# Layer 0's first pass and its hand-overs rewritten: wider runs of x, a hand-made order, weight products inside the pass, early stores, tables in attention's pools

## The chip, the cores and the metric

The kernel runs on one core of one Trainium2 chip. Times are microseconds of device time for one execution. Engines are named as the profile names them: PE is TensorE's matmul side and PEld its weight loads, DVE is VectorE, ACT is ScalarE, POOL is GpSimd, and SP is SyncE, which issues nearly all DMAs in one queue, in order. A matmul holds one operand still (the weights, `lhsT`) and streams the other (`rhs`) through it.

## What is computed

x is a float32 image of 256 by 256 tokens with 128 channels (32 MB). Four layers follow one another, each of the form x = x + f(gn(x)), where gn is a group norm over the whole image. Only layer 0 and the start of layer 1 matter here.

```python
def _gn(v, G=32, eps=1e-5):
    g = v.reshape(B_, H_, W_, G, C_ // G)
    m = jnp.mean(g, axis=(1, 2, 4), keepdims=True)
    s = jnp.var(g, axis=(1, 2, 4), keepdims=True)
    return ((g - m) / jnp.sqrt(s + eps)).reshape(v.shape)
...
def _L0_conv_ref(x, mask, ln_w, ln_b, w_tri, w_q, w_k, w_v, w_g, b_g, w_o, b_o):
    xn = (x - mu) * jax.lax.rsqrt(var + EPS) * ln_w + ln_b      # per token, over 128 channels
    tri_bias = jnp.einsum('bijd,dh->bhij', xn, w_tri)[:, None]
    mask_bias = INF * (mask[:, :, None, None, :] - 1.0)
    q = (xn @ w_q).reshape(B, I, J, H, C) * (1.0 / np.sqrt(C))  # k, v and the gate g alike
    scores = jnp.einsum('bimhc,binhc->bihmn', q, k) + tri_bias + mask_bias
    attn = jax.nn.softmax(scores, axis=-1)
    o = jnp.einsum('bihmn,binhc->bimhc', attn, v)
    return (g * o).reshape(B, I, J, H * C) @ w_o + b_o
...
x = x + _L0_conv_ref(_gn(x), ...)   # layer 0: attention along each of the 256 rows, 4 heads of 32
x = x + _L1_conv_ref(_gn(x), ...)   # layer 1: gated products of tokens, a triangle product
```

The group norm's mean and variance need all of x before the first normalised value exists. So layer 0 reads x once for the statistics and again for the work.

## The kernel before

The kernel keeps channels on the 128 partitions and tokens along the free axis. x arrives with tokens on partitions, so it is turned. Tokens go in 32 pieces of 2,048 (`SC`, 1 MB each); 512 tokens (`CK`) fill one PSUM bank of 2 KB per partition.

**First pass (L209 to L226).** For each piece, SP loads 1 MB of x (L214; each partition gets four runs of 2 KB), PE turns it in 16 transposes of 128x128 (L221, four for each PSUM bank), DVE takes `bn_stats` of the bank (L223) and ACT copies the bank to SBUF (L224). The last 14 pieces (18 to 31, `held`) stay in SBUF. The first 18 are stored to `xT` in DRAM (L226). Tile pools give the loads three buffers (tag `xt`), the copies three (tag `xs`) and PSUM six banks. The order on each engine is made by the framework's scheduler, which sends loads and stores in groups of four.

**Products of weights (L228 to L275).** Layer norm's scale and offset are folded into the weights of layers 0 and 2, in some 20 small matmuls and DVE copies through the pool `f0ps`. They stand behind the first pass, between the last `bn_stats` and the group norm.

**Group norm (L164 and `gn_groups`, L166 to L184).** `bn_aggr` joins the 128 groups of statistics, two small matmuls sum over the channels of a group, ACT takes the root and DVE the reciprocal. The folded weights `wf` and `wt` are scaled by it (L296 to L298).

**Second pass (L316 to L342).** Held and stored pieces alternate (`order`: 18, 0, 19, 1, ...), 32 in all. ACT squares the normalised piece (L321), PE forms five rows of it with `wt` (L324) and sums the squares into one bank (L342), DVE copies the rows out (L330), and SP stores them in four small DMAs (L336, `triD`). For a held piece SP also stores the 1 MB to `xT` (L332), for another it loads one of the next 1 MB pieces (L285, three buffers). The engines' order is written by hand here (`manual_schedule`).

**Hand-over to attention (L349 to L430).** The variance of each token is worked out from the two sums (L353 to L358), written to `rsD` and read back in two layouts. In the pool `p2i`, the bias table `triT` and the mask table `mbT` are loaded, scaled and turned by PE (L382 to L402). Only when `p2i` is closed do attention's pools open, and the first group of rows is loaded (L428, L430), normalised by ACT and POOL (L436, L437) and projected by PE (L464). From there to 1540 us the attention loop runs, unchanged by the diff.

**Hand-over to layer 1 (L638 to L720).** After attention the statistics are checked and joined, and small weights are folded (L664 to L697, pools `f1` and `f1ps`), among them `bz` and `wzc` from eight POOL selections. Then layer 1's first pass loads x1 in pieces of 1 MB (L707) and multiplies (L712). One piece in four is kept in SBUF.

Of the kernel before, what the change touches and what calls it, by code (L numbers as in the profile page):

```python
# [15 lines left out]
P = 128  # L16
# [15 lines left out]
def kernel(ctx: ExitStack, tc: tile.TileContext, a: dict, out: bass.AP):  # L32
# [127 lines left out]

    def gn_finish(stats, name):

        mv = const.tile([P, 2], F32, name=name + "_mv")
        nc.vector.bn_aggr(mv, stats.rearrange("p n s -> p (n s)"))  # L164
        return gn_groups(mv, name)
# [38 lines left out]
    w0c = const.tile([P, 4 * D + NH], F32, name="w0c")  # L204
    slide = const.tile([P, 63], F32, name="slide")
# [3 lines left out]
    with tc.tile_pool(name="x0", bufs=1) as xres, tc.tile_pool(name="p0", bufs=3) as sb:  # L209
        held = {s: xres.tile([P, SC], F32, name=f"x0_{s}") for s in range(RES, NSC)}  # L210
        with tc.tile_pool(name="p0ps", bufs=6, space=PSUM) as ps:
            for s in range(NSC):
                xt = sb.tile([P, 4, 4, D], F32, name="p0_x", tag="xt")
                nc.sync.dma_start(  # L214
                    xt, x_tok[s * SC : (s + 1) * SC, :].rearrange("(c p k) d -> p c k d", p=P, k=4)
                )
                xc = held[s] if s in held else sb.tile([P, SC], F32, name="p0_xc", tag="xs")
                for c in range(4):
                    pt = ps.tile([P, P, 4], F32, name="p0_t")
                    for k in range(4):  # L220
                        nc.tensor.transpose(pt[:, :, k], xt[:, c, k, :], ident)  # L221
                    pf = pt.rearrange("p n k -> p (n k)")
                    nc.vector.bn_stats(stats0[:, s * 4 + c, :], pf)  # L223
                    nc.scalar.copy(xc[:, c * CK : (c + 1) * CK], pf)  # L224
                if s not in held:
                    nc.sync.dma_start(xT[:, s * SC : (s + 1) * SC], xc)  # L226

        with tc.tile_pool(name="f0", bufs=1) as fsb, tc.tile_pool(name="f0ps", bufs=1, space=PSUM) as ps:  # L228
            cen = fsb.tile([P, P], F32, name="f0_c")
            nc.vector.tensor_scalar(cen, ident, -1.0 / D, None, ALU.add)  # L230
            wa = fsb.tile([P, 4 * D + NH], F32, name="f0_a")
            nc.vector.tensor_scalar(wa, w0, ln_w, None, ALU.mult)
            wb = fsb.tile([P, 4 * D + NH], F32, name="f0_b")
            nc.vector.tensor_scalar(wb, w0, ln_b, None, ALU.mult)
            for lo, hi in ((0, 4 * D), (4 * D, 4 * D + NH)):
                pc = ps.tile([P, hi - lo], F32, name="f0_pc", tag=f"f0_pc{lo}")
                nc.tensor.matmul(pc, lhsT=cen, rhs=wa[:, lo:hi], start=True, stop=True)
                nc.vector.tensor_copy(w0c[:, lo:hi], pc)
            pq = ps.tile([P, 3], F32, name="f0_pq")
            for j, i in enumerate((0, 1, 3)):  # L240
                nc.tensor.matmul(pq[:, j : j + 1], lhsT=w0[:, i * D : (i + 1) * D], rhs=ln_b, start=True, stop=True)
            nc.vector.tensor_copy(cqkg, pq)
            pv = ps.tile([P, D], F32, name="f0_pv")
            nc.tensor.matmul(pv, lhsT=ones, rhs=wb[:, 2 * D : 3 * D], start=True, stop=True)
            for k in range(4):
                nc.vector.tensor_copy(cv[:, k, :], pv)

            w2c_ = const.tile([P, 6, D], F32, name="w2c_")
            wa2 = fsb.tile([P, 6, D], F32, name="f0_a2")
            nc.vector.tensor_scalar(wa2[:, 0:5, :], w2[:, 0:5, :], lniw, None, ALU.mult)  # L250
            nc.vector.tensor_scalar(wa2[:, 5, :], w2[:, 5, :], lnow, None, ALU.mult)
            for lo, hi in ((0, 4), (4, 6)):
# [6 lines left out]
            for i in range(6):  # L259
                nc.tensor.matmul(  # L260
                    pb2[:, i : i + 1], lhsT=w2[:, i, :], rhs=lnib if i < 5 else lnob, start=True, stop=True
                )
# [1391 lines left out]
```

## Time and profile before

The median of three runs is 3493.68 us (3490.01 to 3493.93). The profiled execution took 3508.45 us, of which its instructions span 3506.8; it is 14.8 us (0.4%) above the median.

| What | In the profile |
|---|---|
| PE busy | 3133.7 us, 89% of the span, 20260 matmuls and 20260 weight loads |
| DVE, ACT, POOL busy | 66%, 56%, 46% |
| DMA | 759.49 MB, 217 GB/s on the mean |
| first pass, to the last statistics | 0 to 164.1 us |
| weight products and group norm | 164.1 to 175.3 us |
| second pass | 175.3 to 277.4 us |
| hand-over to the first projection | 277.4 to 309.6 us |
| attention | 309.6 to 1540.5 us |
| to layer 1's first matmul | 1540.5 to 1562.9 us |
| layers 1 to 3 | from there to 3506.8 us |

Busy time is the time in which an engine's instructions ran, and matmuls are pipelined, so a busy PE need not be at its peak. In the profile a float32 matmul that is not a transpose stands as two records, each with its own weight load: L464 is issued 384 times and has 768 records. A transpose stands as one: L221 is issued 512 times and has 512. "PEclk" is the TensorE clock granted, as a share of full speed; "DMA share" is the busy share of the core's 16 DMA engines.

### The profile page before, as it was taken

To read this page: it belongs to the slowest core of one execution; us is meant where nothing else is said; L and a number is where in the kernel's file an instruction comes from. 1 tells how busy PE (TensorE), PEld (TensorE's weight loads), DVE (VectorE), ACT (ScalarE), POOL (GpSimd) and SP (SyncE) were. 2 spreads that over 40 slices of the span, in tenths; PEclk is the share of its full clock that TensorE was granted. 3 is DMA by queue.
4 is the path that set the end of the run, shared out by engine and by line. 5 is a ranking of instruction groups with operands and counts; after the bars stand their busy time and mean duration, and the time that the engine had idled before them with its cause. 6 is when DMAs were issued, how large, how long until landed. Compare 5 with 4: busy or idle time off the path is not lost.

```text
span 3506.8 us, 52443 instructions
## 1 busy us (share of the span) xinstructions
PE 3133.7 (89%) x20260; PEld 1652.1 (47%) x20260; DVE 2321.5 (66%) x2637; ACT 1961.4 (56%) x2198; POOL 1605.4 (46%) x821
## 2 busy tenths in 40 slices
PE   3675999999999999966597899999999999959998
PEld 3512555555555555521432344444899533314444
DVE  4624888888888888852388454544555677747776
ACT  3563777777777777733243454443444466636655
POOL 4002777777777777732488000000555354514343
PEclk7887999999999999978799899999999999969999
DMA  9883333333333333349599686775999899747664
GB/s 334 324 317 113 98 123 114 106 122 115 105 122 111 109 122 112 108 156 387 173 321 356 228 312 244 284 270 193 342 353 351 307 335 322 277 168 204 193 200 133
DMA packets 309867, 759.49 MB, mean 217 GB/s; under 512 B 77627, under 2 KB 148957, under 8 KB 259437
## 3 DMA queue, kind: packets, MB, share of 16 engines
q1 hardware_dynamic: 298749, 746.43, 60.9%
q0 software_dynamic: 10864, 9.65, 0.9%
q8 instruction: 162, 2.65, 0.3%
q14 instruction: 92, 0.75, 0.1%
HBM read 468.28 MB, written 287.66 MB: 216 GB/s over the span
## 4 chain that ended last, share of the span: by engine, by line
PE 38%; DMA 7%; DVE 2%; ACT 1%; SPq 1%; issue 1%; POOL 0%; ACTq 0%; DVEq 0%; POOLq 0%
PE p_pm L946 13%; PE tp_z L1612 6%; PE p_pm L1099 4%; PE p_pm L1334 4%; PE p_pg L810 3%; DMA x3T<-p_x 2%; PE tp_a L1601 2%; PE p_st L903 1%; PE p_pt L1371 1%; PE p_pz L818 1%; DMA p_er<-eD 1%; DMA x2T<-p_x 1%; DMA p_x<-x3T 1%; PE p_eb L860 1%; PE p_rz L860 1%
## 5 line engine op out<-in xcount | busy, mean ns | idle before, releaser
L489 DVE TENSOR_TENSOR p_e<-p_S,triT 128x1024 f32<-128x1024 f32 x512 | 609.0, 1211 | 144.7 <-PE p_S L479 144.7
L499 POOL TENSOR_TENSOR p_es<-p_e 128x1024 f32<-128x1024 f32 x256 | 603.1, 2367 | 127.4 <-issue 67.3
L497 ACT ACTIVATE p_e<-p_e,mbT 128x1024 f32<-128x1024 f32 x512 | 551.8, 1137 | 63.0 <-DVE p_e L489 61.2
L946 PE MATMUL p_pm<-p_zn,wf 128*128 128x512 f32 x1040 | 450.0, 594 | 1.4 <-DVE p_zn L963 1.4
L464 PE MATMUL p_mm<-p_xn,wf 128*128 128x512 f32 x768 | 409.2, 617 | 9.2 <-POOL p_xn L437 9.2
L437 POOL TENSOR_TENSOR p_xn<-p_xn,p_rs 128x1024 f32<-128x1024 f32 x64 | 153.5, 2398 | 452.2 <-DMA p_rs<-rsD 259.9
L946 PEld LDWEIGHTS p_pm<-p_zn,wf 128*128 128x128 f32 x1040 | 197.6, 191 | 254.6 <-issue 247.8
L479 PE MATMUL p_S<-p_q,p_k 32*128 32x256 f32 x4096 | 295.4, 400 | 5.0 <-DVE p_e L489 5.0
L479 PEld LDWEIGHTS p_S<-p_q,p_k 32*128 32x128 f32 x4096 | 185.8, 184 | 161.5 <-PE p_mm L455 91.7
L1348 POOL TENSOR_TENSOR p_q<-p_q,p_pb 128x2024 f32<-128x2024 f32 x32 | 144.1, 4503 | 254.8 <-DVE p_pb L1342 254.8
L1612 PE MATMUL tp_z<-p_B,tp_at 128*128 128x256 f32 x1024 | 250.2, 387 | 2.4 <-DMA p_B<-bD 2.2
L512 PE MATMUL p_o<-p_e,p_v 128*32 128x256 f32 x4096 | 249.2, 384 | 0.0
L1012 POOL DMA_DIRECT2D rs__18024<-rs2D x4 | 2.1, 520 | 531.7 <-PE p_pm L946 531.7
L1055 POOL TENSOR_TENSOR k<-k,p_sq 128x512 f32<-128x512 f32 x128 | 163.1, 1274 | 135.2 <-ACT p_sq L1053 135.2
L1165 POOL TENSOR_TENSOR p_x<-p_x,p_g 128x2048 f32<-128x2048 f32 x30 | 136.2, 4542 | 171.9 <-DVE p_g L1152 137.8
L1612 PEld LDWEIGHTS tp_z<-p_B,tp_at 128*128 128x128 f32 x1024 | 185.1, 191 | 24.5 <-issue 2.5
L464 PEld LDWEIGHTS p_mm<-p_xn,wf 128*128 128x128 f32 x768 | 126.8, 191 | 114.6 <-issue 90.3
L1054 DVE TENSOR_TENSOR k<-tp_z,k 128x512 f32<-128x512 f32 x128 | 88.6, 692 | 128.4 <-ACT p_sq L1053 128.4
L512 PEld LDWEIGHTS p_o<-p_e,p_v 128*32 128x32 f32 x4096 | 120.4, 110 | 110.1 <-ACT p_g L470 41.5
L979 DVE SCALAR_TENSOR_TENSOR p_b<-p_pm,b2w,p_b 128x1024 f32<-128x1024 f32 x64 | 82.2, 1284 | 126.6 <-PE p_pm L946 112.2
L455 PEld LDWEIGHTS p_mm<-wf,p_xn 128*128 128x128 f32 x1024 | 135.3, 192 | 62.8 <-issue 61.9
L1051 ACT COPY p_K<-tp_z 128x512 f32<-128x512 f32 x128 | 74.9, 585 | 159.7 <-PE tp_z L1612 159.7
(353 smaller groups left out, 5903.8 us busy)
## 6 DMA issues: line engine op xcount, KB each, us to landing
p_x<-x2T SPq DMA_DIRECT2D x64, 1024.0 KB
p_x<-x1T SPq DMA_DIRECT2D x48, 1024.0 KB
p_x<-in_x_dram SPq DMA_DIRECT2D x32, 1024.0 KB
p_x<-xT SPq DMA_DIRECT2D x64, 512.0 KB
p_rs<-rsD SPq DMA_DIRECT2D x64, 512.0 KB
p_rb<-rzD SPq DMA_DIRECT2D x256, 128.0 KB
x1T<-p_x SPq DMA_DIRECT2D x64, 512.0 KB
aD<-p_a SPq DMA_DIRECT2D x32, 1024.0 KB
```

Of the source, the lines that this page charges most:

```text
L437: nc.gpsimd.tensor_tensor(xn, xn, t["rs"], ALU.mult)
L464: nc.tensor.matmul(pm, lhsT=w, rhs=t["xn"][:, cs_], start=True, stop=True)
L479: nc.tensor.matmul(Ss[h // 2][:, h % 2, u, :], lhsT=t["k"][hp, r * N + u * P : r * N + (u + 1) * P], rhs=t["q"][hp, r * N : (r + 1) * N], ...
L489: nc.vector.tensor_tensor(e[:, :, 2 * p : 2 * p + 2, :].rearrange("p u h n -> p h u n"), Ss[p], triT[:, 2 * p : 2 * p + 2, :, :], ALU.add,)
L497: nc.scalar.activation(e[:, u, :, :], e[:, u, :, :], AF.Exp, bias=mbT[:, u, i : i + 1])
L499: nc.gpsimd.tensor_tensor(es, e[:, 0, :, :], e[:, 1, :, :], ALU.add)
L512: nc.tensor.matmul(t["o"][hp, r % 2, :], lhsT=t["v"][:, r * 2 + u, hp], rhs=e[:, u, h, :], start=(u == 0), stop=(u == 1),)
L946: nc.tensor.matmul(pm[:, c, :], lhsT=wf2[:, i, :], rhs=zns[s][:, k * CK : (k + 1) * CK], start=True, stop=True)
L1055: nc.gpsimd.tensor_tensor(k2, k2, sq, ALU.add)
L1099: nc.tensor.matmul(pm[:, c, :], lhsT=w, rhs=src[:, k * CK : (k + 1) * CK], start=True, stop=True)
L1348: nc.gpsimd.tensor_tensor(q[:, :, 1 : N - 2], q[:, :, 1 : N - 2], pb[:, :, 0 : N - 3], ALU.add)
L1612: nc.tensor.matmul(pz[:, t, :], lhsT=at[:, u, t * P : (t + 1) * P], rhs=Bc[:, u, :], start=(u == 0), stop=(u == 1))
```

## The change

The first pass is written anew in a hand-made order. A piece is loaded as two blocks of 1,024 tokens, so that each partition's run is 4 KB. Three loads go ahead, and the load of piece s+3 is issued after piece s's PE work. A PSUM tile has two banks (three such tiles, in place of six of one bank), and holds 1,024 tokens whose order within the tile has a stride of eight. A turn of 128 tokens would cross the two banks, so it is done as two plain matmuls, with x as weights and one half of the identity (64 columns) as the moving operand: 32 matmuls for a piece in place of 16 transposes, 1,024 in all in place of 512. ACT copies both banks in one instruction. `bn_stats` stays at one bank.

The weight products (`folds`) are issued after piece 12's work, through two PSUM banks of their own, and with them layer 1's `bz` and `wzc`. The statistics of the first 124 groups are joined while the last piece is worked on (`gn_part`), and joined with the last four afterwards (`gn_merge`).

Held pieces 18 to 22 are stored to `xT` ahead of the group norm instead of within the second pass. The variance's offset and square become one ACT instruction. The tables `triT` and `mbT` are built in attention's own pools, so that on SP the first two loads of x for attention and the first `p_rs` go ahead of `tri`, `mk` and `rs`. Nothing else is changed: the attention loop and layers 1 to 3 have the same instructions.

```diff
+    def gn_part(stats, lo, hi, name):
+        mv = const.tile([P, 2], F32, name=name)
+        nc.vector.bn_aggr(mv, stats[:, lo:hi, :].rearrange("p n s -> p (n s)"))
+        return mv
...
+    def gn_merge(a, b, wa, name):
+        mv = const.tile([P, 2], F32, name=name)
+        d = const.tile([P, 2], F32, name=name + "_d")
+        nc.vector.tensor_tensor(d[:, 0:1], a[:, 0:1], b[:, 0:1], ALU.subtract)
+        nc.vector.scalar_tensor_tensor(mv[:, 0:1], d[:, 0:1], wa, b[:, 0:1], ALU.mult, ALU.add)
+        nc.vector.scalar_tensor_tensor(d[:, 1:2], d[:, 0:1], wa * (1 - wa), d[:, 0:1], ALU.mult, ALU.mult)
+        nc.vector.scalar_tensor_tensor(d[:, 1:2], a[:, 1:2], wa, d[:, 1:2], ALU.mult, ALU.add)
+        nc.vector.scalar_tensor_tensor(mv[:, 1:2], b[:, 1:2], 1 - wa, d[:, 1:2], ALU.mult, ALU.add)
+        return mv
...
-        with tc.tile_pool(name="p0ps", bufs=6, space=PSUM) as ps:
+        with tc.tile_pool(name="p0ps", bufs=3, space=PSUM) as ps, tc.tile_pool(
+            name="f0ps", bufs=2, space=PSUM
+        ) as fps, tc.manual_schedule():
+            xts = {}
+            def load0(s):
+                if s < NSC:
+                    xts[s] = sb.tile([P, 2, 8, D], F32, name="p0_x", tag="xt")
+                    nc.sync.dma_start(
+                        xts[s], x_tok[s * SC : (s + 1) * SC, :].rearrange("(c p k) d -> p c k d", p=P, k=8)
+                    )
+            def folds():
+                scratch = sb.tile([P, SC], F32, name="f0_s", tag="xs")
+                at = 0
+                def part(n):
+                    nonlocal at
+                    at += n
+                    return scratch[:, at - n : at]
+                cen = part(P)
+                nc.vector.tensor_scalar(cen, ident, -1.0 / D, None, ALU.add)
+                wa = part(4 * D + NH)
+                nc.vector.tensor_scalar(wa, w0, ln_w, None, ALU.mult)
+                wbv, wbt = part(D), part(NH)
+                nc.vector.tensor_scalar(wbv, w0[:, 2 * D : 3 * D], ln_b, None, ALU.mult)
+                nc.vector.tensor_scalar(wbt, w0[:, 4 * D :], ln_b, None, ALU.mult)
+                for lo, hi in ((0, 4 * D), (4 * D, 4 * D + NH)):
+                    pc = fps.tile([P, hi - lo], F32, name="f0_pc", tag="f0")
+                    nc.tensor.matmul(pc, lhsT=cen, rhs=wa[:, lo:hi], start=True, stop=True)
+                    nc.vector.tensor_copy(w0c[:, lo:hi], pc)
+                pq = fps.tile([P, 3], F32, name="f0_pq", tag="f0")
+                for j, i in enumerate((0, 1, 3)):
+                    nc.tensor.matmul(pq[:, j : j + 1], lhsT=w0[:, i * D : (i + 1) * D], rhs=ln_b, start=True, stop=True)
+                nc.vector.tensor_copy(cqkg, pq)
+                pv = fps.tile([P, D], F32, name="f0_pv", tag="f0")
+                nc.tensor.matmul(pv, lhsT=ones, rhs=wbv, start=True, stop=True)
+                for k in range(4):
+                    nc.vector.tensor_copy(cv[:, k, :], pv)
+                wa2 = part(6 * D).rearrange("p (w d) -> p w d", d=D)
+                nc.vector.tensor_scalar(wa2[:, 0:5, :], w2[:, 0:5, :], lniw, None, ALU.mult)
+                nc.vector.tensor_scalar(wa2[:, 5, :], w2[:, 5, :], lnow, None, ALU.mult)
+                for lo, hi in ((0, 4), (4, 6)):
+                    pc = fps.tile([P, (hi - lo) * D], F32, name="f0_pc2", tag="f0")
+                    nc.tensor.matmul(
+                        pc, lhsT=cen, rhs=wa2[:, lo:hi, :].rearrange("p w d -> p (w d)"), start=True, stop=True
+                    )
+                    nc.vector.tensor_copy(w2c_[:, lo:hi, :].rearrange("p w d -> p (w d)"), pc)
+                pb2 = fps.tile([P, 6], F32, name="f0_pb2", tag="f0")
+                for i in range(6):
+                    nc.tensor.matmul(
+                        pb2[:, i : i + 1], lhsT=w2[:, i, :], rhs=lnib if i < 5 else lnob, start=True, stop=True
+                    )
+                nc.vector.tensor_tensor(b2w, b2w, pb2, ALU.add)
+                pb2 = fps.tile([P, TAPS + 1], F32, name="f0_ps", tag="f0")
+                nc.tensor.matmul(pb2[:, :TAPS], lhsT=ones, rhs=w1[:, :TAPS], start=True, stop=True)
+                nc.vector.tensor_copy(wsum, pb2[:, :TAPS])
+                pk = pb2[:, TAPS : TAPS + 1]
+                nc.tensor.matmul(pk, lhsT=w2c, rhs=b2, start=True, stop=True)
+                nc.vector.tensor_scalar(kcol[:, 0:1], b2, -1.0, None, ALU.mult)
+                nc.vector.scalar_tensor_tensor(kcol[:, 1:2], pk, -1.0, b2, ALU.mult, ALU.subtract)
+                nc.vector.scalar_tensor_tensor(kcol[:, 2:3], b2, 2.0, pk, ALU.mult, ALU.add)
+                pt_ = fps.tile([P, NH], F32, name="f0_pt", tag="f0")
+                nc.tensor.matmul(pt_, lhsT=ones, rhs=wbt, start=True, stop=True)
+                nc.vector.tensor_copy(ctri, pt_)
+                pb = fps.tile([P, 1], F32, name="f1_z", tag="f0")
+                nc.tensor.matmul(pb, lhsT=wz0, rhs=ln2b, start=True, stop=True)
+                nc.vector.tensor_add(bz, pb, bz0)
+                cen4 = part(P).rearrange("p (q c) -> p q c", c=32)
+                nc.vector.memset(cen4, -1.0 / 16)
+                for q in range(4):
+                    nc.gpsimd.affine_select(
+                        out=cen4[:, q, :], in_=cen4[:, q, :], compare_op=ALU.is_ge, fill=0.0, base=-32 * q,
+                        pattern=[[0, 32]], channel_multiplier=1,
+                    )
+                    nc.gpsimd.affine_select(
+                        out=cen4[:, q, :], in_=cen4[:, q, :], compare_op=ALU.is_ge, fill=0.0, base=32 * q + 31,
+                        pattern=[[0, 32]], channel_multiplier=-1,
+                    )
+                nc.vector.tensor_tensor(cen4.rearrange("p q c -> p (q c)"), cen4.rearrange("p q c -> p (q c)"), ident, ALU.add)
+                nc.vector.tensor_scalar(wz4, wz4, g4, None, ALU.mult)
+                pw = fps.tile([P, D], F32, name="f1_w", tag="f0")
+                nc.tensor.matmul(pw, lhsT=cen4.rearrange("p q c -> p (q c)"), rhs=wz4, start=True, stop=True)
+                nc.vector.tensor_copy(wzc, pw)
+            for s in range(3):
+                load0(s)
             for s in range(NSC):
-                xt = sb.tile([P, 4, 4, D], F32, name="p0_x", tag="xt")
-                nc.sync.dma_start(
-                    xt, x_tok[s * SC : (s + 1) * SC, :].rearrange("(c p k) d -> p c k d", p=P, k=4)
-                )
+                xt = xts.pop(s)
                 xc = held[s] if s in held else sb.tile([P, SC], F32, name="p0_xc", tag="xs")
-                for c in range(4):
-                    pt = ps.tile([P, P, 4], F32, name="p0_t")
-                    for k in range(4):
-                        nc.tensor.transpose(pt[:, :, k], xt[:, c, k, :], ident)
-                    pf = pt.rearrange("p n k -> p (n k)")
-                    nc.vector.bn_stats(stats0[:, s * 4 + c, :], pf)
-                    nc.scalar.copy(xc[:, c * CK : (c + 1) * CK], pf)
+                for c in range(2):
+                    pt = ps.tile([P, 2, P // 2, 8], F32, name="p0_t")
+                    for k in range(8):
+                        for h in range(2):
+                            nc.tensor.matmul(
+                                pt[:, h, :, k], lhsT=xt[:, c, k, :], rhs=ident[:, h * 64 : (h + 1) * 64],
+                                start=True, stop=True,
+                            )
+                    for h in range(2):
+                        nc.vector.bn_stats(
+                            stats0[:, s * 4 + 2 * c + h, :], pt[:, h, :, :].rearrange("p n k -> p (n k)")
+                        )
+                    nc.scalar.copy(
+                        xc[:, c * 2 * CK : (c + 1) * 2 * CK], pt.rearrange("p h n k -> p (h n k)")
+                    )
+                load0(s + 3)
                 if s not in held:
                     nc.sync.dma_start(xT[:, s * SC : (s + 1) * SC], xc)
-        with tc.tile_pool(name="f0", bufs=1) as fsb, tc.tile_pool(name="f0ps", bufs=1, space=PSUM) as ps:
...
+                if s == 12:
+                    folds()
+                if s == NSC - 2:
+                    mv_first = gn_part(stats0, 0, T // CK - 4, "gn0_a")
...
-        m0, r0 = gn_finish(stats0, "gn0")
+        early = range(RES, RES + 5)
+        for s in early:
+            nc.sync.dma_start(xT[:, s * SC : (s + 1) * SC], held[s])
+        mv0 = gn_merge(
+            mv_first, gn_part(stats0, T // CK - 4, T // CK, "gn0_b"), 1.0 - 4.0 * CK / T, "gn0_mv"
+        )
+        m0, r0 = gn_groups(mv0, "gn0")
...
-                    if s in held:
+                    if s not in held:
+                        fetch(i)
+                    elif s not in early:
                         nc.sync.dma_start(xT[:, s * SC : (s + 1) * SC], xc)
-                    else:
-                        fetch(i)
...
-            nc.vector.tensor_scalar(mean, mean, off[:, 4:5], None, ALU.add)
-            nc.vector.tensor_tensor(mean, mean, mean, ALU.mult)
+            nc.scalar.activation(mean, mean, AF.Square, bias=off[:, 4:5])
...
-        with tc.tile_pool(name="p2i", bufs=1) as sb, tc.tile_pool(name="p2ips", bufs=2, space=PSUM) as ps:
-            tri = sb.tile([P, NH, 2, N], F32, name="tri")
...
+            tri = eb.tile([P, NH, 2, N], F32, name="tri", tag="p2_e")
+            nc.sync.dma_start(
+                tri.rearrange("p h t n -> p (h t) n"),
+                triD[:NH, :].rearrange("h (t p n) -> p (h t) n", p=P, n=N),
+            )
+            mk_rs = eb.tile([P, 2, 2, N], F32, name="p2_mr", tag="p2_es", bufs=5)
+            mk, rs = mk_rs[:, 0], mk_rs[:, 1]
+            nc.sync.dma_start(mk, mbD.rearrange("(t p) n -> p t n", p=P))
+            nc.sync.dma_start(rs, rsD.rearrange("o (t p n) -> p (o t) n", p=P, n=N))
...
+                pt = psM.tile([P, 2, N], F32, name="p2i_t", tag="p2_mm")
...
             load(0)
+            by_hand.enter_context(tc.manual_schedule())
             prepare(0)
...
-        pb = ps.tile([P, 1], F32, name="f1_z")
-        nc.tensor.matmul(pb, lhsT=wz0, rhs=ln2b, start=True, stop=True)
-        nc.vector.tensor_add(bz, pb, bz0)
-        cen = sb.tile([P, 4, 32], F32, name="f1_c")
...
```

## The prediction, made before the changed kernel was run

> **What bounds the kernel now.** I read three views in this order: busy time by stage, who waited for whom in the first pass, and the weight loads of single lines. Times count from the span's start.
>
> The first view is the busy time of the engines in stretches cut at the stage borders (columns: stretch, its length, busy microseconds and instructions of each engine, clock granted to PE, DMA share, GB/s).
>
> ```profile
> core 0: us, PE busy (x) PEld busy (x) DVE busy (x) ACT busy (x) POOL busy (x), PEclk, DMA share, GB/s
> 0.00:112.40 112.40, 44.69 (x273) 42.09 (x274) 45.76 (x86) 38.99 (x67) 35.27 (x73) 0.72 0.93 335
> 112.40:164.10 51.70, 33.80 (x241) 31.27 (x240) 38.69 (x62) 35.73 (x61) 0.00 (x0) 0.88 0.96 344
> 164.10:175.30 11.20, 8.43 (x38) 6.39 (x38) 7.82 (x22) 2.13 (x4) 0.00 (x0) 0.75 0.47 198
> 175.30:277.40 102.10, 71.18 (x514) 18.90 (x514) 23.89 (x47) 65.26 (x32) 0.00 (x0) 0.84 0.83 306
> 277.40:309.60 32.20, 5.06 (x24) 3.88 (x21) 11.90 (x14) 1.87 (x2) 2.34 (x1) 0.58 0.38 116
> ```
>
> The first pass (two rows: roughly the stored pieces, then the held ones) keeps the DMA engines at 0.93 and 0.96, and PE at 40% and 65%. So it is bound by DMA, at 5.9 us for a stored piece ((112.4 - 6.5) / 18) and about 3.1 for a held one. The second pass is bound by DMA too, after a slow start. In the gap between them DMA is half idle.
>
> The second view, who waited for whom up to 164.1 us (total, times, longest), agrees: PE's largest wait is for x.
>
> ```profile
> PE p_t L221 <- DMA p_x<-in_x_dram: 73.1, 13, 13.6
> SPq L226 <- ACT p_xc L224: 49.0, 18, 6.8
> ```
>
> The third is the timeline of weight loads, three excerpts in which PE runs at full clock (start, busy, count).
>
> ```profile
> 151.28 1.73 PEld L221 LDWEIGHTS p_t<-ident,p_x 128*128 128x128 f32 x16 [0.92 <-ACT x L224]
> 169.79 1.08 PEld L260 LDWEIGHTS f_pb<-L_conv_ln_in_b_sb,w 128*128 128x128 f32 x9
> 1500.00 0.86 PEld L455 LDWEIGHTS p_mm<-wf,p_xn 128*128 128x128 f32 x7 [0.24 <-issue]
> ```
>
> With it go the durations of single ones, from the rows of these lines (shortest/median/longest in ns).
>
> ```profile
> L221 PEld LDWEIGHTS p_t<-ident,p_x x512: 137/143/231, 6.4 to 162.3; 128*128 128x128 f32 x171
> L260 PEld LDWEIGHTS f_pb<-L_conv_ln_in_b_sb,w x10: 191/192/243, 169.5 to 170.7; 128*128 128x128 f32 x10
> L260 PE MATMUL f_pb<-L_conv_ln_in_b_sb,w x10: 167/250/250, 169.8 to 170.7; 128*128 128x1 f32 x10
> L455 PEld LDWEIGHTS p_mm<-wf,p_xn x1024: 190/192/337, 312.3 to 1500.7; 128*128 128x128 f32 x171
> ```
>
> The pace of a row is its busy time less the last load, over the number of steps. Transposes (L221): (1.73 - 0.14) / 15 = 0.106 us each. Plain products with 128 weight columns: L260, which streams one column, (1.08 - 0.192) / 8 = 0.111; L455, which streams 128, (0.86 - 0.192) / 6 = 0.111. The pace is the same for 1 and for 128 streamed columns, so the weight load sets it.
>
> **The change, part by part.**
>
> *The turning of x.* A plain float32 product has two records with a weight load each, a transpose has one. The 512 transposes become 1,024 products, so 512 loads become 2,048. Their 64 streamed columns lie between the 1 of L260 and the 128 of L455, both at 0.111, so I take 0.111: 64 records x 0.111 = 7.1 us for a piece, against 5.9 and 3.1 for DMA. PE becomes the bound of the whole pass: 2048 x 0.111 = 227.3 us. The bounds from rows: 0.106 (the transposes' pace) to 0.165 (a load of 0.111 and then a stream of 64 columns, half of the 0.107 of 128, without overlap); as L455 overlaps fully, I stay at the lower side.
>
> A rule speaks against this edit as well. The Trainium skill, "TensorE: Matmul & The Clock Gate", section Terms, says that the transpose mode is four times faster for float32; by it the 512 x 0.106 = 54 us of transposes would become 217. The same page's section "Back-to-back issue gap" prices matmuls of 1 to 64 columns at about 25 ns, which would make 51 us of the 2,048 and leave DMA the bound; L260's row, with one column at 0.111, contradicts that for these weight loads.
>
> *The end of the first pass.* First x at 6.5 us, as now (same 1 MB ahead); 227.3; 1.5 more for a start at half clock (the first sixteen transposes now take 3.25 us in place of 1.94); the last tile's statistics, 1.6 (two of 0.69 and handing over). To that come the weight products, which now stand in PE's queue between pieces 12 and 13, so that pieces behind them wait: two statistics, `cen` and `wa` before they can begin (2.1), the chain itself, 7.8 as now (164.75 to 172.6), about 3 more because two PSUM banks serve all of it and `wa2` is made within it, and 2.5 for `bz`, the eight selections on POOL (two rows of 0.72, in a queue that is empty after 45 us), two DVE products and `f_w`. That is 15.4, and 1.5 for a clock that drops meanwhile. Sum: 6.5 + 227.3 + 1.5 + 1.6 + 15.4 + 1.5 = 253.8, against 164.1: **+89.7**. Bounds of the stall: 7.8 and 20.
>
> Nothing else in this pass costs: DMA needs 2.1 MB per 7.1 us, 295 GB/s, under the 335 of the row; the runs of 4 KB therefore gain nothing (in the trace's DMA packets the commonest 2 KB packet takes 84 ns and the commonest 4 KB one 159, so a load could lose 5%). DVE's four statistics take 2.8 a piece and ACT's two copies about 2.3 (no row for 1,024 columns out of PSUM; L497's 1.14 is nearest). SP issues load s+3 behind piece s's PE work, two pieces or 14 us ahead of need. The early `bn_aggr` (3.6 us) lies beside PE. Were PE not the bound, all these would lie beside DMA.
>
> *The gap.* Now 11.2 us: `bn_aggr` 3.6, the products 8, then 2.5 from `gn_pm` to the first square. After: a small `bn_aggr` and five small DVE steps at 0.16 to 0.22, 1.3 in all, 0.3 of handing over, and the same 2.5: 4.1, **-7.1**.
>
> *The second pass.* SP's queue loses five stores here; one of them (18) is already issued at 155 us, so four of 13 leave the pass. In its bound part a pair of pieces, one load and one store, takes 6.1 us (squares of loaded pieces start at 239.5, 245.6 and 251.7), so four stores are 12.2. The five early ones, and the three first loads for this pass, go out while PE ends the first pass, where DMA has room; the mask's load, queued behind them, waits for the group norm's end as it does now. **-13**, between -8 (the early pairs fall to the squares' pace of 4.0, which several already have) and -21 (DMA at its full rate throughout).
>
> *The hand-over.* On SP, `p_x` (two loads) and `p_rs` now pass `tri`, `mk` and `rs`. Now `tri` is loaded early and `rs` lands at 293.9; after it come 7.3 us of scaling and turning, then the loads, then ACT and POOL, and PE projects at 309.6. After: `rsD` written at about 290.7 (0.4 saved by one ACT step for two DVE steps), then 2 MB in one queue, at 340 GB/s 6.2, and 2 of latency: `rs` at about 299; 6.5 us of turning as now, which stands ahead of the projection in PE's queue; projection at about 305.1. POOL's product is done at 298.5 and waits. **-4.5**, between -1 and -6.
>
> *Layer 1's start.* Today the first kept piece is loaded only at 1557.5, behind `wzc` (the pool `f1` lies where it goes), and PE starts at 1562.9. Without `f1` it goes third in the queue from 1547.8: 3 MB at 345 GB/s and 2 of latency give 1559. **-3.5**, between 0 and -7.5 (where `v` would be the last).
>
> **Sum:** 89.7 - 7.1 - 13 - 4.5 - 3.5 = +61.6. Against the profiled execution's own 3508.45 that is 3570; the median of the runs is 14.8 lower, so 3493.7 + 61.6 = **3555**.
>
> **The rivals.** A: the forecast, PE bound by weight loads. Its own range: 0.108 a load (-6), a stall of 9 (-6), the savings at their ends (-14) give 3530; the other ends, 0.112, a stall of 20, small savings and some windows at half clock, give 3583.
>
> B, the other side: the load of a 64-column product is not what I read, and DMA stays the bound. For it: within the transposes' bursts the second load starts 58 ns after the first, so a load can be that short. Against it: in every plain product with 128 weight columns, at least 0.108. Then a stored piece stays at DMA's pace or gains the 5% of its load, the stall is covered by three loads ahead, held pieces take 64 x 0.057 = 3.6 in place of 3.1, and the pass ends some 5 us earlier: -5 - 28 = -33, 3460. It decides at the pace where 26.5 + 2048 p = 164.1 + 28.1, p = 0.081 us.
>
> C, slower still: the clock. Where it is granted at half, the steps are 0.213 (L244, 166.75 to 166.96). With PE streaming only half of the time, it might stay there: +209, 3764; or the stream does not overlap the load, 0.165: +110, 3666. Against it: L455 and L260 at full clock, and the clock is 1.00 where PE is 58% busy (135 to 155 us).
>
> D: the change doesn't do what it says, in that the savings don't come: 3583 is its end in A.
>
> **How the numbers follow.** A 0.84, of which 0.80 lie within 3530 to 3583; B 0.08; C 0.06; 0.02 for a pace near 0.081 and no change. A measurement here tells about 0.2%, 7 us, from no change. Faster 0.08, same 0.02, slower 0.90. The range is A's own.
>
> **What would show it.** Right: 2,048 records of the new product line in a pass that ends near 254 us, PE's wait for x almost gone, a step of 0.111 between weight loads, DMA share near 0.8 and then 0.4, a PE hole of 10 us or more after piece 12, a gap of 4 us, a second pass of about 89. Wrong: steps below 0.081, or a pass that still ends near 164 with PE waiting for x.

## The result, and the profile after

The changed kernel takes 3787.32 us (median of four runs, 3775.60 to 3807.55) against 3493.80 for the kernel before (median of four, 3490.01 to 3522.23): a ratio of 1.083, 95% interval 1.075 to 1.090. The forecast was 3555. Its profiled execution took 3775.6 us, span 3773.9; that of before 3508.45 and 3506.8. The stages from the two traces, in us:

| stage | before | after | difference | forecast |
|---|---|---|---|---|
| first pass, to the end of its last statistics | 164.1 | 462.6 | +298.5 | +89.7 |
| gap, to the first square | 11.3 | 5.1 | -6.2 | -7.1 |
| second pass, to its last product | 102.1 | 104.6 | +2.5 | -13 |
| hand-over, to the first projection | 32.2 | 26.6 | -5.6 | -4.5 |
| layer 1's start | 22.5 | 20.6 | -1.9 | -3.5 |
| the rest, whose code is the same | | | -20.2 | 0 |
| span | 3506.8 | 3773.9 | +267.1 | +61.6 |

The medians differ by 26 more than the spans because the profiled execution of before was 14.7 above its median and that of after 11.7 below. (The last row but one is taken up at the end of the point-by-point section.)

The busy time by stage of the changed kernel, with the columns of the first view of before:

```profile
core 0: us, PE busy (x) PEld busy (x) DVE busy (x) ACT busy (x) POOL busy (x), PEclk, DMA share, GB/s
0.00:462.56 462.56, 447.78 (x2086) 444.12 (x2086) 93.98 (x167) 65.08 (x64) 36.64 (x81) 0.71 0.37 134
462.56:467.65 5.09, 1.17 (x4) 1.00 (x4) 1.91 (x13) 2.56 (x4) 0.00 (x0) 0.50 0.00 0
467.65:572.23 104.58, 72.50 (x514) 19.50 (x514) 23.90 (x47) 65.37 (x32) 0.00 (x0) 0.82 0.72 259
572.23:598.82 26.59, 3.86 (x22) 3.57 (x21) 9.33 (x11) 2.48 (x3) 2.34 (x1) 0.61 0.56 179
```

PE is busy 97% of the first pass and DMA 37%: PE has become the bound, as forecast. But the pass is twice as long as PE's 2,048 records were to make it. Why is in the durations of the product's line (shortest/median/longest in ns, then the first and last start; the tail is the shape and how many sampled records have it):

```profile
L332 PEld LDWEIGHTS p_t<-ident,p_x x2048: 288/333/337, 6.1 to 460.7; 128*128 128x128 f32 x187
L332 PE MATMUL p_t<-ident,p_x x2048: 314/421/447, 6.1 to 460.8; 128*128 128x64 f32 x187
```

A weight load of 128 by 128 took 192 ns (median) in the plain products that the forecast was made from. Here the median is 333, from the first to the last; the median step from one load to the next is 0.213 us, the 5th and the 95th percentile 0.213 and 0.214. That is the step of L244 in the kernel before (from 166.75 to 166.96 us), where its trace records the half clock. The turn's products waited once for x, 6.1 us for the first; the clock did not stay up in 455 us of work broken only by the weight products.

The page's clock row hides this:

```profile
PEclk9955588999999999999888989999999999979999
```

Its first slices of 94 us each say full speed. The trace holds changes of the clock only. In this trace the first is at 195.2 us: full, for 3.4 us, right behind weight products of 512 and 256 columns (L279, 192.2 to 195.1 us), and then half again from 198.6 until 471.7. So from piece 13 on (201.7 us) the half clock is on record, and load and step are the same there as before it. What lies before the first change is filled in as full; the load of 333 ns says that it was half. The 0.71 in the table above has the same fault. So the shown clock was 1.00 where it was half, and only the step tells.

### The profile page after: what moved, and what is told of

It is laid out like the page before. It is cut to its first block, busy times and chain, and to the rows that moved or that the text cites. A ratio compares the mean times of both kernels' runs of the same rounds, so it can differ in the third digit from the quotient of the medians.

```text
span 3773.9 us, 55529 instructions
## 1 busy us (share of the span) xinstructions
PE 3479.4 (92%) x21796; PEld 2011.4 (53%) x21796; DVE 2323.4 (62%) x2642; ACT 1953.7 (52%) x2135; POOL 1606.2 (43%) x821
## 5 line engine op out<-in xcount | busy, mean ns | idle before, releaser
L332 PE MATMUL p_t<-ident,p_x 128*128 128x64 f32 x2048 | 437.2, 421 | 6.1 <-DMA p_x<-in_x_dram 6.1
L332 PEld LDWEIGHTS p_t<-ident,p_x 128*128 128x128 f32 x2048 | 437.1, 333 | 6.1 <-issue 6.1
L337 DVE BATCH_NORM_STATS2 stats<-p_t 128x6 f32<-128x512 f32 x128 | 82.9, 690 | 356.6 <-PE p_t L332 356.6
L506 PEld LDWEIGHTS p_mm<-p_xn,wf 128*128 128x128 f32 x768 | 126.1, 191 | 104.6 <-issue 89.4
```

The lines of the kernel that those rows point to most:

```text
L332: nc.tensor.matmul(pt[:, h, :, k], lhsT=xt[:, c, k, :], rhs=ident[:, h * 64 : (h + 1) * 64], start=True, stop=True,)
L506: nc.tensor.matmul(pm, lhsT=w, rhs=t["xn"][:, cs_], start=True, stop=True)
```

## The experiments

**Is it the turn?** First the changed kernel with its transposes back:

```diff
-   for k in range(8):
-       for h in range(2):
-           nc.tensor.matmul(pt[:, h, :, k], lhsT=xt[:, c, k, :], rhs=ident[:, h * 64 : (h + 1) * 64], ...)
+   for k in range(8):
+       nc.tensor.transpose(pt[:, k // 4, :, k % 4], xt[:, c, k, :], ident)
...
+   # the copy to xc reads pt as "p h n k" and writes "p (n h k)"
```

> The changed kernel with one edit undone: x is turned by 512 transposes again (eight for 1,024 tokens, four into each of two PSUM banks); runs of 4 KB, order, early weight products, early stores and the rest stay. Theory 1, the half products alone are the loss: the first pass is bound by DMA again and ends between 150 and 166 us (462.6 with the half products, 164.1 before); with what the two traces show for the other stages (gap -6.2, second pass +2.5, hand-over -5.6, layer 1's start -1.9) the whole is 3493.8 - 11 and up to 14 less, 3468 to 3486. Theory 2, the order by hand or the weight products in the middle of the pass hold PE or its clock: the pass still ends later than 200 us and the whole lies above 3520.

Measured: 3479.94 us, ratio to before 0.994 (0.992 to 0.997). The first pass ends at 160.3, the gap is 5.1, the second pass 102.7, the hand-over 27.0. Theory 1 holds. Everything but the turn makes the kernel some 20 us faster.

The other way round, the kernel before with only the turn changed:

```diff
-   nc.tensor.transpose(pt[:, :, k], xt[:, c, k, :], ident)
+   for h in range(2):
+       nc.tensor.matmul(pt[:, h * 64 : (h + 1) * 64, k], lhsT=xt[:, c, k, :],
+                        rhs=ident[:, h * 64 : (h + 1) * 64], start=True, stop=True)
```

> The kernel before with one edit: each transpose is two products of 64 columns of the identity; runs of 2 KB, planner's order and all else as before. Theory 1: the turn alone holds the clock at half, 2,048 records at 0.2133 us, the first pass ends at about 6.5 + 437 + 2 = 445 us in place of 164 and the whole is about 3775. Theory 2, it takes the other parts too: the clock comes up, 0.111 a record, the pass ends near 240 and the whole is about 3570, or nearer to before.

Measured: 3785.08 us, ratio 1.079 (1.075 to 1.083); the pass ends at 444.1, 280 us later than before, and the median step is again 0.213. So the turn makes 280 of the 298.5; the other 18.4 are about what the weight products held PE up: in the trace of after piece 12 begins at 170.0 us, every piece takes 13.65, and piece 13 begins at 201.7, 18.0 late.

**Why does the clock stay at half?** Two kernels tell the share of streaming from the kind of product. One uses whole products (128 columns, half as many), the other keeps 64 columns and takes them from x, which is dense:

```diff
-   rhs=ident[:, h * 64 : (h + 1) * 64]     # 16 products for 1,024 tokens
+   rhs=ident                               # 8 products, as eight transposes would lie
```

> The changed kernel with the turn done by plain products of 128 columns of the identity, 512 of them, 1,024 records: as many weight loads as streams of 128 columns. Theory 1a, what counts for the clock is how much of the time PE streams (half of it with 64 columns behind each load of 128): here it streams all the time, the clock comes up, 0.111 us a record, 114 us in all, DMA binds and the pass ends at 150 to 170; the whole 3468 to 3490. Theory 1b, a plain product with the identity, nearly all zeros, doesn't count whatever its length: half clock, 1024 x 0.2133 = 218 us, the pass ends near 245 and the whole is 3787 - 218 = about 3570.

```diff
-   rhs=ident[:, h * 64 : (h + 1) * 64]
+   rhs=xt[:, c, k, h * 64 : (h + 1) * 64]
```

> The changed kernel with the 64 moving columns taken from x itself in place of the identity, as many records of the same size (x is not turned, so that all that follows works on other numbers). Theory 1a, the share of streaming decides: the clock stays at half, the pass ends near 462 us, the whole about 3787. Theory 1b, the zeros of the identity decide: full clock, 2048 x 0.111 = 227 us, the pass ends near 254 and the whole is about 3580.

The same rows of both, whole products first:

```profile
L331 PEld LDWEIGHTS p_t<-ident,p_x x1024: 186/192/338, 6.0 to 173.5; 128*128 128x128 f32 x171
```

```profile
L332 PEld LDWEIGHTS p_t<-p_x x2048: 288/333/333, 5.9 to 462.4; 128*128 128x128 f32 x187
```

With 128 columns of the same identity the clock comes up at 8.9 us, the median step is 0.112 and the pass ends at 177.0; the whole is 3497.36, ratio 0.999 (0.996 to 1.002). With 64 dense columns nothing changes: 464.2 and 3785.03. It isn't the identity's zeros, and it isn't the plain product. (The pass with whole products is 7 us longer than theory 1a had it, and the whole lies 7 above. Its clock went back to half from 73.7 to 97.6 us, around the weight products; the rest was not followed up.)

Two more keep the number of records at 2,048 and raise the columns, to 96 and to twice 128:

```diff
-   for h in range(2):
-       nc.tensor.matmul(pt[:, h, :, k], ..., rhs=ident[:, h * 64 : (h + 1) * 64])
+   for lo in (0, 32):
+       nc.tensor.matmul(pt[:, k // 4, lo : lo + 96, k % 4], ..., rhs=ident[:, lo : lo + 96])
```

> The changed kernel with 96 moving columns in each product in place of 64 (columns 0 to 95 and 32 to 127 of the identity, so that 64 columns of each turn are written twice with the same values); 2,048 records as in the changed kernel, half as many columns again. If the share of streaming decides the clock and three quarters are enough: full clock, 2048 x 0.111 = 227 us, the first pass ends at 240 to 260, the whole about 3787 - 209 = 3578. If three quarters are not enough: 437 us, 3787. In between if the clock alternates.

```diff
+   for _ in range(2):
+       nc.tensor.matmul(pt[:, k // 4, :, k % 4], lhsT=xt[:, c, k, :], rhs=ident, start=True, stop=True)
```

> The changed kernel with every turn done twice, each by a plain product of 128 columns: 2,048 records as in the changed kernel, twice the columns. It is the forecast's own sum with the clock that it took for granted. Theory 1: full clock, 0.111 a record, the first pass ends at 245 to 258 us and the whole lies at 3555 to 3585, some 210 below the changed kernel though it streams twice as much. Theory 2, the number of weight loads without a pause keeps the clock low: half clock, 437 us, about 3787.

The load and the product with 96 columns:

```profile
L332 PEld LDWEIGHTS p_t<-ident,p_x x2048: 191/192/337, 5.9 to 256.4; 128*128 128x128 f32 x187
L332 PE MATMUL p_t<-ident,p_x x2048: 274/275/501, 5.9 to 256.5; 128*128 128x96 f32 x187
```

and the load with twice 128:

```profile
L332 PEld LDWEIGHTS p_t<-ident,p_x x2048: 192/192/338, 5.9 to 257.3; 128*128 128x128 f32 x187
```

The clock comes up at 10.2 and 11.5 us and stays up but for 17 us around the weight products, the median step is 0.112 in both, the pass ends at 258.1 and 259.0, and the whole is 3586.58 (ratio 1.022, 1.013 to 1.032) and 3579.51 (1.020, 1.012 to 1.029), two runs each. The changed kernel with every turn done twice, with twice the streamed columns, is 208 us faster than the changed kernel itself. So for products that each reload 128 by 128 weights without a pause, 64 columns leave the clock at half and 96 bring it up. At full clock records of 512 columns follow each other at 0.429 us (L464 in the attention loop of before, where PE does not wait), so 64 columns are an estimated 0.054 us, about half of a step of 0.112, and 96 an estimated 0.080, nearly three quarters. Whether this share decides or the number of columns behind each load, the runs can't tell: both change together.

**The second pass.** The forecast wanted 13 us from four stores that leave it (the traces have 13 of them in the pass before and 9 after), since DMA seemed to bind it. In the changed kernel DMA's share there is 0.72 and in the kernel with the transposes 0.80: DMA does not bind all of it. The largest wait there is VectorE's, for small stores to `triD` to land. First guess, more buffers for them:

```diff
-   tr = wk_sb.tile([P, CK], F32, name="p1_tr", bufs=3)
+   tr = wk_sb.tile([P, CK], F32, name="p1_tr", bufs=5)
```

> The kernel with the transposes back (3479.9, its second pass 102.7 us), with one number changed: five buffers for `tr` in place of three. Theory 1: the second pass is paced by the small stores to `triD`, for whose landing VectorE's copies wait 62.9 us of the pass (the largest wait there); with five buffers these waits fall below 30 us, the fetches go out earlier and the pass takes 80 to 95 us, the whole 3458 to 3473. Theory 2, the forecast's: DMA's bytes bind it; the waits move to the loads and the pass stays at 100 to 105.

Measured: 3480.64 us, the second pass 107.7, VectorE's wait still 54.4 us. Theory 1 was wrong; but theory 2 doesn't fit either, with 107.7 against its 100 to 105 and a DMA share of 0.74. SP's timeline of the changed kernel shows more (start, us, line, operation; `x8` stands for eight transfers):

```profile
476.65 0.36 SPq L359 DMA_DIRECT2D p_xc<-xT  x1
477.06 5.23 SPq L416 DMA_DIRECT2D triD<-p_tr  x8
482.40 0.36 SPq L359 DMA_DIRECT2D p_xc<-xT  x1
482.86 5.03 SPq L416 DMA_DIRECT2D triD<-p_tr  x8
488.00 0.36 SPq L359 DMA_DIRECT2D p_xc<-xT  x1
```

Load, eight small stores, load. By the trace's semaphore events SP's transfers use eight semaphores in turn, and each first waits for the transfer eight places before it. Seven small stores go out 0.3 us apart; the eighth waits (from 485.2 to 487.6) until the load in front of them, whose packets run from 483.4 to 487.3 and whose last semaphore event is at 487.6, is in. In this stretch only one load is under way at a time. The kernels that test this stand on one with transposes and spread weight products (told at the end of this section; 3462.74 us, second pass 101.0); one edit was also made to the kernel before. All small stores on another queue:

```diff
-   nc.sync.dma_start(triD[:, s * SC + c * CK : s * SC + (c + 1) * CK], tr[32 * c : 32 * c + 5, :])
+   nc.gpsimd.dma_start(triD[:, s * SC + c * CK : s * SC + (c + 1) * CK], tr[32 * c : 32 * c + 5, :])
```

> The kernel with transposes and the weight products handed out in steps (3462.7, second pass 101.0 us), with one edit: the 128 small stores to `triD` go out on GpSimd's DMA queue, idle in this pass, in place of SP's. In the trace SP's transfers take eight semaphores in turn (101 to 103 and 114 to 118), so a transfer waits until the one eight before it has landed; a pair of pieces has one load and eight of these stores, nine transfers, so each load of 1 MB has to land before the next pair's is issued (issued at 482.40, landed at 486.9; next one at 488.00). Theory 1, that is what paces the pass: without the small stores in the row, loads run three ahead, the pass falls to ScalarE's 4.1 us a pair or DMA's 2.7 to 6, 78 to 90 us in all, and the whole to 3440 to 3452. Theory 2, DMA's bytes bind the pass, as the forecast had it: 99 to 104 us as before.

> The kernel before with the same edit alone (small stores to `triD` on GpSimd's queue); its second pass, 102.1 us with DMA at 0.83, has thirteen 1 MB stores where the changed kernel has eight. Theory 1: the row of eight paces it here too, it gains, but by less, as the five stores more need 5 x 2.6 us of DMA: 88 to 97 us. Theory 2, DMA's bytes bind it: 100 to 104.

Measured: 95.2 us for the pass on top of the new kernel, 97.6 on top of before. In the first kernel pairs follow each other at 3.9 to 4.7 us from 177.8 to 199.0, near ScalarE's two squares, as theory 1 has it; without the edit they take 5.5 to 5.6 (175.3 to 197.6). DMA has gaps without the edit and is full with it (first line without):

```profile
170.00:200.00 30.00, 21.94 (x184) 6.50 (x187) 7.60 (x11) 22.61 (x12) 0.00 (x0) 0.95 0.74 262
```

```profile
170.00:200.00 30.00, 20.58 (x160) 5.69 (x160) 5.54 (x8) 23.15 (x12) 18.48 (x38) 0.83 0.99 372
```

But these pairs live in part on three loads issued from 170.0 to 171.1 us, during a hole of 9.5 us without the start of a square (166.3 to 175.8). And the small stores land no sooner: VectorE waits 65 us for them there, and the hand-over grows from 28.6 to 32.5 and from 32.2 to 39.8. In the second kernel, where nearly every pair has a load and a store, pairs still take 5.8 to 7.2 us from 198.5 to 230.1, and DMA is full:

```profile
200.00:210.00 10.00, 4.82 (x44) 0.90 (x36) 2.08 (x3) 6.51 (x4) 5.95 (x12) 1.00 1.02 416
```

So once the row does not hold the transfers, DMA binds pairs with a load and a store, as the forecast had it. The whole is 3482.57 (ratio 0.995, 0.992 to 0.998) and 3503.22 (1.000, 0.997 to 1.003): no gain. On top of the new kernel the two passes gain 8 us in the profile and the hand-over loses 4; 19.5 more are lost behind the first projection, in code that is the same, which no run explains. Neither theory's number was met. (The changed kernel's pass has nine 1 MB stores, not the eight of the expectation.)

The five early stores put back:

```diff
-   early = range(RES, RES + 5)
+   early = range(0)
```

> The kernel with transposes and spread weight products (second pass 101.0 us) with the five early stores back in the second pass, on SP between the others. By the forecast, DMA binds this pass at 3.05 us a store: 101 + 13 = about 114, and the gap stays. By the theory of the row of eight: a pair has ten transfers in place of nine and one more load or store of 2.6 us that partly lies beside the small ones; 101 to 106.

Measured: 105.9 against 101.0 us, the whole 3462.92 against 3462.74. The pass lies inside what the row of eight gives (101 to 106), and 8 us under the forecast's 114; the whole is unchanged. The 5 us themselves are from one trace each, and the seven kernels with the same second pass as the changed one took 97.5 to 104.6.

The last one makes the row shorter and moves the mask, whose store held SP at the pass's start, to GpSimd's queue:

```diff
-   tr = wk_sb.tile([P, CK], F32, name="p1_tr", bufs=3)
-   nc.vector.tensor_copy(tr, pr)
+   if s in held or s + RES >= NSC:
+       tr = wk_sb.tile([P, 2, CK], F32, name="p1_tr", bufs=2)
+   nc.vector.tensor_copy(tr[:, int(s in held), :], pr)
...
+   # behind the loaded piece alone, four stores for both pieces of the pair (the last four have no partner)
+   nc.sync.dma_start(pieces[:, s : s + RES + 1 : RES, col], tr[32 * c : 32 * c + 5, :, :])
...
-   nc.sync.dma_start(mk, ...); nc.sync.dma_start(mbD..., mk)
+   nc.gpsimd.dma_start(mk, ...); nc.gpsimd.dma_start(mbD..., mk)
```

> The kernel with transposes and the weight products handed out in steps (3462.7, second pass 101.0 us), with two edits. The two pieces of a pair share one `tr` of two halves and leave it by four small stores in place of eight, so that a pair takes five transfers of SP's row of eight, six with a 1 MB store. And the mask's load and store go out on GpSimd's queue: in the run with all small stores there, SP stood at the mask's store until 169.5 us and no load was issued from 155.8 to 170.0 (hole of 9.5 us between two squares at 166.3 and 175.8). Theory 1, the row of eight and the mask's place pace this pass: pairs at 4.1 us without a store and at about 5.8 with one, 85 to 93 us in all, the whole 3445 to 3458. Theory 2, taking the small stores out of the row only moves the wait, to VectorE's copies that wait for their landing (65 us of waits in that run): 95 to 102 us, the whole 3455 to 3470.

Measured: 3452.82 us, ratio to before 0.987 (0.981 to 0.992); second pass 87.9. The 30 us after its start, without and with the two edits:

```profile
160.00:190.00 30.00, 22.81 (x190) 6.30 (x182) 6.65 (x10) 22.21 (x12) 0.00 (x0) 0.94 0.57 188
```

```profile
160.00:190.00 30.00, 28.76 (x255) 7.97 (x246) 8.52 (x13) 30.00 (x16) 0.39 (x1) 1.00 0.94 343
```

ScalarE works without a pause (30.00 of 30) and DMA goes from 188 to 343 GB/s. ScalarE is the bound of this stretch; behind it, from 190 to 220 us, pairs take 5.3 to 6.6 us at a DMA share of 0.99 to 1.01, and DMA is. What each of the two edits is worth was not taken apart.

**The weight products in the middle.** With the transposes back, DMA binds the first pass again, and the weight products show as a hole in it:

```profile
70.00:80.00 10.00, 4.37 (x12) 2.96 (x12) 2.92 (x12) 0.60 (x1) 0.00 (x0) 0.53 1.02 423
80.00:90.00 10.00, 7.52 (x24) 5.66 (x24) 2.78 (x12) 0.00 (x0) 1.02 (x6) 0.50 0.09 36
90.00:100.00 10.00, 7.91 (x50) 7.00 (x50) 6.97 (x14) 4.05 (x4) 0.56 (x3) 0.78 0.36 137
100.00:110.00 10.00, 5.67 (x32) 4.99 (x32) 5.03 (x8) 4.06 (x5) 0.00 (x0) 0.74 1.01 386
```

So they were made a generator that gives out one step behind each 1,024 tokens:

```diff
-   scratch = sb.tile([P, SC], F32, name="f0_s", tag="xs")
+   scratch = held[NSC - 1]
...
+   yield                      # behind each group of products and copies
...
+   if s >= 8:
+       next(steps, None)
...
-   if s == 12:
-       folds()
```

> The kernel with the transposes back (3479.9, first pass to 160.3 us), its weight products handed out one step behind each 1,024 tokens from piece 8 on, with the last held piece's buffer as scratch, in place of all of them behind piece 12. There DMA moved 36 and 137 GB/s in the two stretches of 10 us from 80 to 100 us, and about 410 around them. Theory 1, that hole is lost time for a pass bound by DMA: 14 to 18 us come back, the pass ends at 142 to 148 and the whole is 3460 to 3468. Theory 2, VectorE's statistics at the end of the pass (busy 0.95 to 1.0 of the time from 130 us) set its end anyway: it ends at 155 or later and the whole is 3474 or more.

Measured: 3462.74 us, ratio 0.989 (0.983 to 0.995); the pass ends at 147.2. The same stretches:

```profile
70.00:80.00 10.00, 8.14 (x38) 7.76 (x38) 4.95 (x14) 3.56 (x4) 0.00 (x0) 0.53 1.01 417
80.00:90.00 10.00, 6.32 (x36) 5.31 (x34) 7.00 (x14) 4.91 (x6) 1.57 (x8) 0.79 1.02 422
90.00:100.00 10.00, 5.44 (x32) 4.86 (x32) 5.08 (x8) 4.13 (x5) 0.00 (x0) 0.83 1.02 424
```

The hole is gone and DMA stays at 417 to 424 GB/s. 13 us come back, just under theory 1's 14 to 18; the pass's end and the whole lie in its ranges. Handing the products out and taking the scratch out of the copies' buffers (`xs`) weren't taken apart.

## Why the prediction was wrong

**The failed step** is the clock that stands behind "0.111 a record". The forecast read the pace from bursts at full clock and put the half clock among the rivals: "With PE streaming only half of the time, it might stay there: +209, 3764". That is what happened, at 0.06 of the chances for all of rival C: the first pass took 298.5 us more, against 89.7 + 209 = 298.7, and the changed kernel is 208 us slower than the one with every turn done twice, at full clock. The reason given against it was that L455 and L260 run at full clock and that the clock is 1.00 where PE is only 58% busy. Neither excludes it: L455 streams 128 columns for each load, L260 is a burst of ten, and PE's busy share does not say what it streams. Here PE was busy 97% of the time and the clock stayed low. The signs of being wrong that the forecast lists all lie on the fast side.

The Trainium skill, "TensorE: Matmul & The Clock Gate", Part 1, has a table of two states in which the full clock comes after about 3.4 us of sustained busy PE. The trace's changes do come in multiples of 3.4 us, but 455 us of busy PE did not bring it up for good here; the columns streamed for each load decided.

**The rest of the first pass** was right once the clock is. With full clock and the same 2,048 records the pass ends at 258.1 and 259.0, against the 253.8 of the sum, and the wholes of 3580 and 3587 stand against its 3555. PE as the bound, the load as its pace for 96 and 128 columns alike (0.112), and a stall behind piece 12 all hold. The stall was 18.0 us in the changed kernel and 18.0 and 17.9 in these two, against 15.4 in the sum; the drop of the clock around it cost 1.9 and 2.3 more, against 1.5.

**"The runs of 4 KB therefore gain nothing"** holds for the changed kernel, where DMA has room. It was too small for a pass that DMA binds: with transposes and spread weight products the pass ends 16.9 us earlier than before (147.2 against 164.1), at 387 GB/s against about 335 to 344. The runs of 4 KB and the order by hand weren't taken apart.

**The gap**, -7.1 forecast, -6.2 measured, 4.9 to 5.1 us long in every run of the new code: right. **The hand-over**, -4.5 forecast, -5.6: right. **Layer 1's start**, -3.5 forecast, -1.9 measured: inside its bounds, smaller.

**The second pass**, -13 forecast, +2.5 measured, was the other wrong term, and outside its bounds of -8 to -21. The step that failed is "In its bound part a pair of pieces, one load and one store, takes 6.1 us ..., so four stores are 12.2". The 6.1 is near DMA's own pace; but a pair that loses its store does not fall to half of it, nor to the 4.0 of the lower bound. A stretch of before with stores, and one of the changed kernel without:

```profile
205.30:215.30 10.00, 7.26 (x52) 2.11 (x56) 2.12 (x4) 6.10 (x4) 0.00 (x0) 0.83 0.99 371
```

```profile
487.60:497.60 10.00, 7.28 (x64) 2.22 (x64) 2.77 (x4) 8.15 (x4) 0.00 (x0) 1.00 0.63 199
```

Pairs without a store still take 5.5 to 5.8 us in the changed kernel (loads issued at 476.65, 482.40, 488.00, 493.80 and 499.32), at a DMA share of 0.63 in this stretch, so a store less saves an estimated 0.3 to 0.6 us of the 6.1. That the row paces them is shown by SP's waits above, by DMA's share of 0.99 in place of 0.74 with the small stores on another queue, and by the last run: with the row shortened and the mask moved, pairs follow at 4.0 us (160.4 to 188.2) and the pass takes 87.9.

**What stays open:** the work behind the first projection, whose code is the same but for layer 1's start, was 22 us shorter in the profile of after than in that of before, 20 without layer 1's start. In all runs with the code of before it took 3186 to 3197 us, in those with the new code 3172 to 3183, one 3195. Some 16 of the 20 us lie in layers 1 to 3, which took 1932 to 1944 us with the code of before and 1923 to 1946 with the new code, so a spread of single executions may be all of it. No run explains it.

## What to carry to other kernels

Before a rewrite trades transposes for plain products, work out how many columns PE streams for each load of weights, not how busy it is: a float32 product that reloads 128 by 128 weights for 64 columns ran at half clock for as long as it lasted, one with 96 at full. Read the clock from the duration of a known instruction, since the clock row is empty of meaning up to its first change. And before a pass is put down to DMA's bytes, look at the queue that issues its transfers: many small ones in one row can hold the large ones back at a DMA share of 0.6 to 0.8. And ask it for each kind of step by itself: here pairs with a store ran near DMA's bound, and pairs without one were held by the row at nearly the same pace.

## What the runs showed of the hardware that was not expected

- 2,048 records of 64 columns kept the weight loads busy for 437 us, 2,048 of 96 columns for 233, and of 128 columns for 234. More work per record took little more than half the time.
- The clock row was full speed in the page for the first slices of kernels whose weight loads took 333 ns (median) in them; without any change in the trace nothing contradicts it but the durations.
- In the first 110 us, stretches of 10 us with a DMA share of 1.0 or more moved 361 to 388 GB/s before, and 382 to 427 with runs of 4 KB, the order by hand and spread weight products.
